# Reordering the seam between a mixture-of-experts layer, a four-group attention chain and a sparse key-value feed-forward

## The chip, the cores and the metric

The kernel runs as one launch on one core of a Trainium2 chip. The time is the device time of one execution in microseconds. It is given as the median of several runs of the unchanged kernel. All figures of a trace come from one further execution that the hardware profiler recorded.

## The reference, cut to what matters

The input `x` is 16 sequences of 128 tokens with 128 features, and `ctx_1024` has the same shape. Four layers follow each other. Each is a cross-attention over the context and a feed-forward part, and each adds its result to `x`. The change lies in the second half of layer 1 and in layer 2.

- Layer 1's feed-forward part is a mixture of 14 experts with one expert per token: `logits = norm(x) @ router`; each token goes to the expert with the largest logit; there `y = gelu(norm(x) @ w1[e] + b1[e]) @ w2[e] + b2[e]`; and `x += p * y`, with `p` the softmax weight of that expert.
- Layer 2's attention part is a block of its own: it normalises `x`, runs a causal self-attention, normalises, runs an attention over the context, normalises, runs a two-layer perceptron, normalises and adds to `x`. Its scores have one head of 128 features. A sequence's length is the number of scores of its first query that are not zero, and keys beyond that length are masked.
- Layer 2's feed-forward part looks up 1024 small experts: `xn = rms(x)`; `xn` gives 32 + 32 similarities for each of 8 heads; the eight best sums of one similarity of each side are kept per head; `x += (gelu(xn @ down.T) * weights) @ up`, with the kept sums as weights.

## The kernel before

Tokens lie on the 128 partitions. The 16 sequences form four groups of four (`NG = 4`, `GB = 4`), and X stays in SBUF for the whole program. A scheduler puts each engine's instructions into order at build time: it follows the order in which the Python code emits them, and among those it takes what its own cost estimates say is ready first. `tc.issue_after(ins)` adds an edge of order without a wait: what is emitted inside the block and runs on the engine of `ins` is issued behind `ins`.

The stretch in question is the function `layers_1_and_2`. Its pieces are Python generators. Each `next` emits a few instructions and stops at a `yield`, and the function chooses which piece is stepped next.

- `routing(n)` normalises a group, computes the router's logits and marks each token's expert (layer 1, groups 0 to 3).
- `places(k)`: the two halves of the batch (sets 0 and 1, two groups each) are sorted by expert. The function computes each token's row in a table in DRAM and issues eight scatters on GpSimd (line 1064), one per sequence.
- `tiles(k)`: the sorted table has 21 tiles of 128 rows, taken three at a time, so seven steps per set. Each step loads three tiles (`of`, line 1114, from SyncE's queue), copies three experts' weights by a register's value (`wt`, line 1123, on VectorE), runs two matrix products with a gelu between (lines 1134 to 1145), and stores the result (line 1148).
- `back(k)` gathers each token's result with eight indirect transfers on GpSimd (line 1155) and adds it to X on VectorE (line 1104). `biases(k)` adds the experts' second bias, with a small matrix product per group.
- `prepare(n)` computes the context products `k2` and `v2` of one group of layer 2's attention. `chain(n)`, called `attention` by the function that steps it, is the whole attention block of one group, in 34 steps: moments, normalising, query, scores and softmax (`weights`), weighted values, normalising, scores and softmax against the context, values, normalising, perceptron, and the final addition (line 1349). Its reciprocal root runs on GpSimd (line 245). The first two chains take other engines for small sums than the last two, which get `aside`.
- `layer2_ffn`: a prelude multiplies `w_q` with `keys` (`pk`, 16 products, line 1373). `begin(n)` normalises a group and transposes it. `similar(i)` and `thresholds` find the eight best sums of a sequence `i` per head. Then for each of 16 sequences and 8 heads one step builds a grid of 1024 sums on GpSimd (`C`, line 1446), marks the eight best on VectorE (line 1467) and adds the transposed grid into PSUM on TensorE (line 1469). There are 128 such steps. The grids have nine buffers and are emitted four steps ahead.

In the order before, `biases(0)` follows `places(1)` beside the last tiles of set 0. The gathers of set 0 are emitted after that scatter, with no edge between them, and the seven tiles of set 1 are stepped together with a round of `back(0)`, two chains side by side and all four `prepare`, and `biases(1)`. After the tiles, `back(1)` is stepped with the two chains. The prelude of the feed-forward part is emitted, then what is left of both chains. Chains 2 and 3 are stepped one step per head step. `begin(n + 1)` is called at the start of sequence `4n + 1`, and `similar(4n + 4)` at head step 6 of sequence `4n + 2`.

## Time and profile before

| | |
|---|---|
| median of 3 runs | 1454.21 us (1449.42 to 1455.87) |
| the profiled execution | 1458.99 us, span 1457.2 us, mean granted TensorE clock 0.883 |
| TensorE matmul busy | 1196.4 us (82%) |
| TensorE weight load busy | 812.1 us (56%) |
| VectorE busy | 867.9 us (60%) |
| ScalarE busy | 595.6 us (41%) |
| GpSimd busy | 497.0 us (34%) |

The busy shares are means over stages that have different limits, so they do not say what a stage is worth. The stretch of this change runs from about 792 us to 1275 us of the span. A timeline gives an instruction's start and length in us, its engine, its line, what it writes and reads, and in brackets how long the engine had been idle and what it then waited for. Matrix products are issued from one helper (line 232), so they are told apart by the tiles that they write.

### The profile page before, as it was taken

What the parts mean: (1) busy time and instruction counts of PE and PEld (TensorE: products, weight loads), DVE (VectorE), ACT (ScalarE), POOL (GpSimd) and SP (SyncE); (2) the same over time, 40 slices, a digit from 0 to 9 for tenths busy, and PEclk for the clock granted to TensorE, in tenths of its full rate; (3) what the DMA queues carried; (4) which work ended last, traced back from release to release, by engine and by line L of the source; (5) the groups of instructions that cost most, each with busy time, mean ns of one, the idle gap of its engine ahead of it and who ended that gap; (6) DMA issues with size and microseconds to landing.
All of it is one profiled execution on the core that took longest, in us unless ns stands there. A gap on an engine that the chain in (4) does not pass through costs nothing. (4 is left out here: it accounts for less than half of the span.)

```text
span 1457.2 us, 24584 instructions
## 1 busy us (share of the span) xinstructions
PE 1196.4 (82%) x9908; PEld 812.1 (56%) x9948; DVE 867.9 (60%) x2249; ACT 595.6 (41%) x1009; POOL 497.0 (34%) x559
## 2 busy tenths in 40 slices
PE   6887799898989777998777485677998898879986
PEld 2445355454545423555556374567887788825466
DVE  6666456565655676756545222347876888676652
ACT  3444465564655334445433236333334321133331
POOL 3223000000000135544322302169887899742100
PEclk9998799999999877979898578669999999999996
DMA  7000000000000200000012203000000000000000
GB/s 226 2 2 18 0 0 1 0 1 0 1 1 0 81 28 1 2 2 2 2 54 68 60 24 105 1 1 1 1 2 1 10 1 1 1 6 2 2 2 29
DMA packets 27587, 27.06 MB, mean 19 GB/s; under 512 B 3409, under 2 KB 25809, under 8 KB 27089
## 3 DMA queue, kind: packets, MB, share of 16 engines
q1 hardware_dynamic: 22128, 22.08, 4.6%
q0 software_dynamic: 1024, 2.10, 0.5%
q10 hardware_dynamic: 4320, 1.31, 0.4%
q8 instruction: 78, 1.28, 0.4%
q14 instruction: 37, 0.30, 0.1%
HBM read 17.88 MB, written 7.60 MB: 17 GB/s over the span
## 5 line engine op out<-in xcount | busy, mean ns | idle before, releaser
L1446 POOL TENSOR_TENSOR C<-sim 128x1024 f32<-128x1024 f32 x128 | 241.6, 1919 | 26.7 <-PE pc L1469 14.4
L1467 DVE MATCH_REPLACE8 C<-out,C 128x1024 f32<-128x1024 f32 x128 | 154.1, 1209 | 0.0
L232 PE MATMUL pc<-hm,weights_f 128*128 128x512 f32 x320 | 148.3, 595 | 3.0 <-DVE hm L840 2.6
L245 POOL TENSOR_TENSOR rstd<-ve,minus_half 128x4 f32<-128x4 f32 x44 | 44.7, 1017 | 291.8 <-DVE ve L242 277.0
L1469 PE MATMUL pc<-consts,C 128*128 128x128 f32 x1024 | 135.6, 284 | 10.3 <-POOL C L1446 6.2
L1469 PEld LDWEIGHTS pc<-consts,C 128*128 128x128 f32 x1024 | 122.9, 148 | 19.4 <-POOL C L1446 10.9
L461 DVE TENSOR_REDUCE nm<-s 128x8 f32<-128x1024 f32 x96 | 114.0, 1216 | 23.9 <-PE s L232 23.4
L354 POOL MEMSET V<- 128x2560 f32 x6 | 13.4, 2259 | 250.1 <-PE pb L934 236.7
L525 DVE RECIPROCAL inv<-av 128x128 f32<-128x128 f32 x48 | 45.9, 957 | 87.3 <-PE av L232 87.3
L232 PEld LDWEIGHTS pc<-hm,weights_f 128*128 128x128 f32 x320 | 59.9, 190 | 55.5 <-issue 45.7
L605 ACT ACTIVATE pT<-st 128x1024 f32<-128x1024 f32 x64 | 62.3, 1022 | 67.4 <-PE st L232 67.4
L232 PE MATMUL st<-Qb,K 32*128 32x512 f32 x512 | 84.9, 660 | 0.0
L232 PE MATMUL s<-Kb,Q 32*128 32x512 f32 x384 | 75.3, 690 | 6.6 <-ACT pT L533 2.6
L535 POOL TENSOR_TENSOR E<-pT 128x1024 f32<-128x1024 f32 x32 | 60.6, 1910 | 55.8 <-ACT pT L533 55.8
L475 POOL CAST nms<-nm 128x16 bf16<-128x16 f32 x64 | 14.7, 256 | 160.1 <-DVE nm L461 132.5
L232 PEld LDWEIGHTS av<-pT,V 128*32 128x32 f32 x1536 | 42.7, 116 | 39.9 <-issue 24.2
L840 DVE TENSOR_TENSOR hm<-he,M 128x512 f32<-128x512 f32 x64 | 40.7, 685 | 31.2 <-ACT he L836 28.3
L232 PE MATMUL av<-pT,V 128*32 128x128 f32 x1536 | 57.6, 291 | 1.6 <-DVE inv L549 1.2
L533 ACT ACTIVATE pT<-st 128x1024 f32<-128x1024 f32 x32 | 31.3, 1022 | 61.2 <-PE st L232 61.1
L232 PE MATMUL av<-pT,consts 128*32 128x128 f32 x1536 | 53.5, 280 | 0.0
L232 PE MATMUL ph<-xnext,weights_f 128*128 128x256 f32 (+1 forms) x96 | 32.1, 457 | 24.1 <-DVE xnext L893 24.1
L1123 DVE COPY wt<-weights_f 128x514 f32 x42 | 17.6, 426 | 55.7 <-PE po L232 50.6
(365 smaller groups left out, 2637.6 us busy)
## 6 DMA issues: line engine op xcount, KB each, us to landing
weights_f<-in_f SPq DMA_DIRECT2D x1, 3852.5 KB, 11.9
weights_f<-in_f SPq DMA_DIRECT2D x1, 2816.5 KB, 9.7
rows<-zero SPq DMA_DIRECT2D x2, 1344.0 KB, 15.5
of<-rows SPq DMA_DIRECT2D x14, 192.0 KB, 2.5
outs<-rT SPq DMA_DIRECT2D x14, 192.0 KB, 2.0
weights_f<-in_f SPq DMA_DIRECT2D x1, 2351.5 KB, 11.5
X<-in_x ACTq DMA_DIRECT2D x4, 256.0 KB, 9.2
ctx_sb<-in_ctx SPq DMA_DIRECT2D x4, 256.0 KB, 5.6
```

The source lines that it names most:

```text
L232: return nc.tensor.matmul(o, lhsT=lhsT, rhs=rhs, start=start, stop=stop)
L245: nc.gpsimd.tensor_tensor(o, ve, minus_half[:, :w], ALU.pow)
L461: nc.vector.tensor_reduce(nm[:, b, 8 * u : 8 * u + 8], ss[u].rearrange("p r (g k) -> p (r g) k", g=4), AX.X, ALU.max, negate=True,)
L525: nc.vector.reciprocal(y, s)
L533: nc.scalar.activation(E, st, AF.Exp, scale=8.0**-0.5)
L535: nc.gpsimd.tensor_mul(E2, E, E)
L605: nc.scalar.activation(pT, st, AF.Exp)
L840: nc.vector.tensor_mul(hm[:, k, c : c + 2, :], he, M[:, k, c : c + 2, :])
L1123: nc.vector.tensor_copy(wt, table[:, bass.ds(where[r], EW)])
L1446: nc.gpsimd.tensor_add(C, sim[:, h, 0, :].unsqueeze(2).to_broadcast(sh), sim[:, h, 1, :].unsqueeze(1).to_broadcast(sh),)
L1467: nc.vector.match_replace(at, m8[:, h, :], at, 0.0)
L1469: nc.tensor.matmul(pc[:, k // 4, k % 4 * P : (k % 4 + 1) * P], lhsT=C[:, 4 * k : 4 * k + 4, :].rearrange("p i j -> p (i j)"), rhs=ident, s ...
```

## The change

- `back` emits its eight gathers inside an `issue_after` on the last scatter of set 1, so the gathers of set 0 are queued behind that scatter on GpSimd. They are now emitted before `biases(0)`.
- `biases(0)` moves from beside set 0's last tiles to behind those gathers, followed by `prepare(0)` to `prepare(2)`. Then the first step of set 1's tiles is emitted, and then the additions of set 0.
- Each of the other six tile steps of set 1 is followed by three steps of chain 0 and, in the last three, by one step of chain 1. The weights of layer 2's feed-forward part are loaded after that, in two transfers, of which the first holds `w_q` and `keys`.
- The gathers of set 1 are emitted, and `biases(1)`, `prepare(3)` and the additions of set 1 are stepped with seven steps of chain 0.
- The prelude's products are followed by what is left of chain 0 (seven steps), each with a step of chain 1; on TensorE these are queued behind the prelude.
- What is left of chain 1 (22 steps), chain 2 and chain 3 are stepped beside the 128 head steps, one per step and two in one step of eight. Chain 1 gets `aside` as chains 2 and 3 do.
- `begin(n + 1)` moves from the start of sequence `4n + 1` to head step 5 of sequence `4n + 2`, one head step ahead of `similar(4n + 4)`.
- One `yield` in `weights` is gone, so a chain has 32 steps where it had 34.

```diff
-    def load(name):
+    def load(name, parts=()):
...
-        nc.sync.dma_start(t[:, :n], packs[name])
+        cut = [0, *parts, n]
+        for a, b in zip(cut, cut[1:]):
+            nc.sync.dma_start(t[:, a:b], packs[name][:, a:b])
...
+                d["scattered"] = ins
...
-            for at in range(ST):
-                nc.gpsimd.indirect_dma_start(
...
+            with tc.issue_after(state[1]["scattered"]):
+                for at in range(ST):
+                    nc.gpsimd.indirect_dma_start(
...
             nc.vector.tensor_scalar(top, most, -0.1 * BIG, -scale, ALU.max, ALU.mult)
-            yield
             E = tokens("E", 3)
...
-        def chain(n, aside=None):
+        def chain(n, complete, aside=None):
...
+            complete[n] = True
             yield
...
-            mm(pk[:, c * 32 : (c + 1) * 32], w["w_q"][:, c * P : (c + 1) * P],
-               w["keys"][:, c * 32 : (c + 1) * 32])
+            last = mm(pk[:, c * 32 : (c + 1) * 32], w["w_q"][:, c * P : (c + 1) * P],
+                      w["keys"][:, c * 32 : (c + 1) * 32]).ins
...
+        complete["prelude"] = last
...
         def begin(n):
+            assert n in complete
...
             pc = opened(i)
-            if i % GB == 1 and i + GB < NB:
-                begin(i // GB + 1)
...
                 if h == 4:
                     G = gelus(i)
+                if h == 5 and i % GB == 2 and i + GB < NB:
+                    begin(i // GB + 1)
                 if h == 6 and i + 2 < NB:
                     sims[i + 2] = similar(i + 2)
...
-                for _ in together(first, after(routing(NG - 1), places(1), biases(0))):
+                for _ in together(first, after(routing(NG - 1), places(1))):
                     pass
...
-                contexts = [prepare(n) for n in range(NG)]
-                half = together(
-                    attention(0), attention(1), after(*contexts)
-                )
-                second, others = tiles(1), back(0)
+                complete = {}
+                chains = [attention(n, complete, eps if n else None) for n in range(NG)]
+                second, sums = tiles(1), back(0)
+                one(sums)
+                for _ in after(biases(0), prepare(0), prepare(1), prepare(2)):
+                    pass
                 one(second)
-                one(others)
-                for _ in together(second, after(others, pairs(half)), biases(1)):
+                for _ in sums:
                     pass
-                load("f2")
-                others = back(1)
-                one(others)
-                for _ in range(6):
-                    one(half)
-                for _ in others:
-                    one(half)
+                for k in count():
+                    if not one(second):
+                        break
+                    steps(chains[0], 3)
+                    if k > 2:
+                        steps(chains[1], 1)
+                load("f2", [sum(cols["f2"][k][2] for k in ("w_q", "keys"))])
+                sums = back(1)
+                one(sums)
+                for part in (biases(1), prepare(3)):
+                    for _ in part:
+                        steps(chains[0], 1)
+                steps(chains[0], 1)
+                for _ in sums:
+                    steps(chains[0], 1)
             with tc.tile_pool(name="f2w", bufs=2, side="right") as wk:
-                forward = layer2_ffn(wk)
+                forward = layer2_ffn(wk, complete)
                 one(forward)
-                for _ in half:
-                    pass
-                chains = after(attention(2, eps), attention(3, eps))
-                for _ in forward:
-                    if chains and not one(chains):
-                        chains = None
-                        load("a3")
+                with tc.issue_after(complete["prelude"]):
+                    for _ in chains[0]:
+                        steps(chains[1], 1)
+                rest = after(*chains[1:])
+                for at, _ in enumerate(forward):
+                    for _ in range(2 if at % 8 == 3 else 1):
+                        if rest and not one(rest):
+                            rest = None
+                            load("a3")
```

`one(part)` emits one step of a generator, and `steps(part, n)` emits `n`.

More of the change, by code (lines that the diff above doesn't have):

```diff
@@ L1 @@
 import math
+from itertools import count
 from contextlib import ExitStack, nullcontext
@@ L1153, in back @@
             gs = [wk.tile([P, GB, P], F32, name="g", bufs=2) for _ in range(2)]
-            for at in range(ST):
-                nc.gpsimd.indirect_dma_start(
-                    out=gs[at // GB][:, at % GB, :], out_offset=None, in_=d["outs"][:, :],
-                    in_offset=bass.IndirectOffsetOnAxis(ap=d["place"][:, at : at + 1], axis=0),
-                )
+            with tc.issue_after(state[1]["scattered"]):
+                for at in range(ST):
+                    nc.gpsimd.indirect_dma_start(
+                        out=gs[at // GB][:, at % GB, :], out_offset=None, in_=d["outs"][:, :],
+                        in_offset=bass.IndirectOffsetOnAxis(ap=d["place"][:, at : at + 1], axis=0),
+                    )
             yield
@@ L1351, in chain, with layer2_ffn @@
                 )
+            complete[n] = True
             yield
         return prepare, chain
-    def layer2_ffn(wk):
+    def layer2_ffn(wk, complete):
         w = {k: sb[f"f2.{k}"] for k in cols["f2"]}
@@ L1539, in together, with steps @@
                 yield
+        def steps(part, n):
+            for _ in range(n):
+                one(part)
         def after(*parts):
@@ L1543, in after @@
                 yield from part
-        def pairs(part):
-            while one(part):
-                one(part)
-                yield
         with ExitStack() as left:
@@ L1575, in layers_1_and_2 @@
                 )
-                contexts = [prepare(n) for n in range(NG)]
-                half = together(
-                    attention(0), attention(1), after(*contexts)
-                )
-                second, others = tiles(1), back(0)
+                complete = {}
[4 more added lines that the diff above has]
+                    pass
```

## The prediction

> **What bounds the kernel now.** I read the page's slices first: TensorE is busy 7 to 9 tenths almost everywhere, with one dip in slices 23 to 27, where PE shows 4 to 8 and PEclk 5 to 8. So I cut that stretch by its events (last router result, first and last tile of set 1, last gather, end of chains 0 and 1, first marked grid, end of chain 3, last grid) and asked the table of windows. Columns: length; busy us (instructions) of PE, PEld, DVE, ACT, POOL; clock; DMA.
>
> ```profile
> 792.00:817.30 25.30, 6.30 (x25) 4.97 (x25) 12.03 (x55) 0.37 (x1) 17.78 (x18) 0.51 0.20 59
> 817.30:853.00 35.70, 30.07 (x122) 23.29 (x123) 8.71 (x22) 13.08 (x35) 2.53 (x2) 0.60 0.16 45
> 853.00:889.70 36.70, 29.20 (x204) 24.10 (x204) 8.07 (x21) 22.02 (x47) 0.00 (x0) 0.99 0.27 95
> 889.70:905.30 15.60, 6.76 (x32) 5.48 (x32) 5.45 (x30) 6.60 (x25) 8.72 (x9) 0.77 0.17 48
> 905.30:946.40 41.10, 26.30 (x121) 20.84 (x122) 10.89 (x62) 17.44 (x50) 5.68 (x7) 0.67 0.00 1
> 946.40:975.50 29.10, 21.38 (x100) 16.74 (x101) 10.45 (x72) 11.71 (x38) 14.25 (x10) 0.65 0.00 0
> 975.50:1162.70 187.20, 163.06 (x1216) 147.36 (x1227) 145.74 (x478) 70.29 (x168) 159.96 (x94) 0.92 0.01 3
> 1162.70:1274.80 112.10, 99.30 (x788) 94.25 (x794) 89.84 (x274) 15.75 (x30) 98.57 (x57) 0.94 0.01 2
> ```
>
> The first six rows, 183.5 us, are bound by latency: no engine is full, and TensorE runs at 0.51 to 0.67 of its clock in four of them. The last two are the 16 sequences of the feed-forward part, where PE, DVE and POOL are all at 78 to 89%. The first nine sequences, which carry chains 2 and 3, take 187.2 / 9 = 20.8 us each, the last seven 16.0.
>
> The timeline shows why the first row is empty:
>
> ```profile
> 797.32 0.15 DVE L1060 CAST place<-pos 128x8 uint32<-128x8 f32 x1
> ...
> 801.83 0.95 POOL L1155 DMA_INDIRECT g<-outs,place  x1 [0.30 <-issue]
> ...
> 803.08 1.13 POOL L1064 DMA_INDIRECT rows<-xn,place  x1 [0.30 <-DVE X L1104]
> ...
> 812.31 0.97 POOL L1064 DMA_INDIRECT rows<-xn,place  x1 [0.30 <-issue]
> ...
> 817.33 0.87 PE L1127 MATMUL pt<-consts,of 128*128 128x128 f32 x3 [15.74 <-DMA of<-rows]
> ```
>
> The places are known at 797.5, but set 0's gathers hold POOL until 802.8, so the scatter that TensorE waits for starts at 803.1. The seam after the tiles:
>
> ```profile
> 889.17 0.56 DVE L1147 COPY rT<-po 128x384 f32<-128x384 f32 x1 [8.04 <-PE po L232]
> ...
> 901.83 0.49 DVE L252 BATCH_NORM_STATS2 st<-pz 128x6 f32<-128x128 f32 x2
> ...
> 946.50 6.90 PEld L232 LDWEIGHTS pk<-weights_f 128*128 128x128 f32 x32 [4.25 <-DVE X L1349]
> ...
> 965.50 7.51 POOL L1446 TENSOR_TENSOR C<-sim 128x1024 f32<-128x1024 f32 x4 [0.71 <-ACT sim L1414]
> ...
> 975.59 1.21 DVE L1467 MATCH_REPLACE8 C<-out,C 128x1024 f32<-128x1024 f32 x1
> ```
>
> The chains' moments at 901.8 sat in DVE's queue behind additions that waited for gathers. The prelude `pk` came only after both chains, and the first grid is marked 86.4 us after the last tile.
>
> **The change part by part.** The base is the profiled execution, 1458.99 us (span 1457.2). It lies 4.8 above the median of the runs, so I take the difference off the median.
>
> *Scatter.* With the gathers behind it, the scatter starts 0.3 after its places instead of at 803.1: 5.3 us earlier. `biases(0)` also leaves the stretch in which DVE computes the places; its two additions at 794.9 and 797.1 waited in that queue, worth up to 2.5 more. So 5.3 to 7.8; I take 7. The gathers then run about 806 to 816, and chain 0's first reciprocal root behind them at about 816.6; before it came at 813.3 behind the scatter, and its normalising ran at 821.9, so nothing on the path is later.
>
> *Tile stage* (817.3 to 889.7, 72.4 us). Out go four `prepare` (pk at 850.1 and 862.8, pv at 852.9 and 865.6: 2 to 4 us of PE each, some 11 in all) and `biases(1)` (831.1 to 834.5 and 838.7 to 846.4, about 5 of PE). Three `prepare` and `biases(0)` fill PE's 15.7 us wait. In comes chain 0's second half instead of chain 1's first, about the same work. Set 0's tiles at full clock came every 4.7 us (line 1147 at 779.3 and 784.0), which for seven is 33; three chain steps between two tiles, some 2 to 3 us of PE and ACT, make it 44 to 54. If the clock stays where it was, the stage can stay at 72 or, with chain waits in PE's queue, grow by a few us (I allow 4). I take 54, near the row of set 0's tiles, since PE no longer stands still before: 18 us gained, bounds -4 and 28.
>
> This term rests on the clock: the row 817 to 853 had PE busy 30.1 of 35.7 us at 0.60, so 30.1 x 0.4 = 12 us of it is slow clock. [...]
>
> *Last tile to first marked grid* (889.2 to 975.6, 86.4). The gathers and additions after the last tile still take 16 us (889.2 to 905.2); chain 0's steps 19 to 25 fit in it. From the moments to chain 0's last addition the trace has 901.8 to 946.4 for one and a half chain halves of two chains side by side; counted for one chain from moments of the context part on (rows 928.8 to 946.4, 17.6 us), it stays about 17.5, as half the queue is gone but the chain is a string of waits. `pk`, 7.0 us on PE, moves into DVE's and ACT's part of that (moments, root, normalising: 5.5 us); what sticks out, 1.5, I add. Behind it `begin(0)` no longer waits for `keys` (953.6) and `whole`: moments 1.9, small sums and root 2.4, normalising 1.6, transposition and copy 1.3, two products 4.0, copy 0.6, then 965.5 to 975.6 unchanged, 22 in all where the trace has 29. Sum 16 + 17.5 + 1.5 + 22 = 57; seven steps of chain 1 beside it, 3 us. So 60: 26 gained. Bounds 10 (chain 1's steps and `pk` fully in the way) and 35.
>
> *Feed-forward part* (299 us). It now carries 86 chain steps for 68, or 0.69 of a chain more. Chains 2 and 3 cost 9 x (20.8 - 16.0) = 43 us, or, against sequences 9 to 14 (101.6 / 6 = 16.9), 35: 17 to 22 per chain. So 12 to 15 more; I take 13.
>
> *Late `begin`.* Its cover was 13 head steps; now it is one. The rows of `begin(2)`:
>
> ```profile
> 1065.81 1.12 DVE L1349 SCALAR_TENSOR_TENSOR X<-pz,rstd,X 128x128 f32<-128x128 f32 x4 [4.13 <-POOL rstd L245]
> ...
> 1069.13 0.47 DVE L252 BATCH_NORM_STATS2 st<-X 128x6 f32<-128x128 f32 x2
> ...
> 1082.11 0.69 ACT L1389 ACTIVATE xT<-pt,weights_f 128x512 f32<-128x512 f32 x1 [3.66 <-PE pt L293]
> ```
>
> From moments to `xT` are 13.7 us, to the similarities about 16, against some three head steps (7 us) until DVE has their maxima in its queue. The markings of the current sequence sit behind those maxima. Left over are 0 to 9 us per group, three times 0 to 27; with grids computed ahead on POOL and most maxima emitted late, I take 6.
>
> *Small edits.* The two-part load costs one more issue on SP, hidden: the weights were asked for at 874.9 and used at 946.5. The dropped `yield`, and chain 1's `aside` (its small sums go from DVE to ACT, which is 38% busy in the row with chains), I take at nothing; bounds -2 and +3, for without that slack ACT delays the chain, not the grids.
>
> Sum: -7 - 18 - 26 + 13 + 6 = -32: 1427 on the profiled execution, 1422 on the median.
>
> **The rivals.** (a) *The slow clock stays and the gain shrinks.* Tile stage 66 instead of 54, chain 0 as slow as two were: -7 - 6 - 18 + 13 + 6 = -12, so 1442. For it: the clock fell to 0.6 even in busy windows. Against: set 0's tiles ran at 1.00 after a full stretch.
>
> (b) *Slower: `begin` holds the marking queue.* Chain 1 must end before `begin(1)`. Chain 2 took from 961.8 to 1066.9 for 32 steps, 3.3 us each, while head steps without chains take 2.0. Where DVE stands at each of three group changes for the whole 16 us of `begin` and similarities, that is 48; with 13 for the steps it is 61 against a front gain of 51, or of 31 as in (a): +10 to +30, 1464 to 1484. It decides from about 13 us per group change on. For it: `[4.13 <-POOL rstd]` shows such a stand. Against: POOL holds grids ahead, and the order is chosen by readiness.
>
> (c) *It doesn't do what it says*: the scheduler already places chain steps where engines are free, and the tiles stay bound by ScalarE's gelu hand-offs; only the scatter's 7 and the seam's low bound of 10 remain, and the feed-forward part takes 13 back: -4, so 1450.
>
> **How the numbers follow.** Forecast 0.57; its best ends (tile stage 44, seam 35, no late `begin`: -7 - 28 - 35 + 12 = -58, 1396) another 0.06; (a) 0.13; (c) 0.08; (b) 0.16. This measurement can tell about 0.5%, 7.3 us, from no change, so faster means below 1446.9. The forecast, its best end and most of (a) are faster, 0.74; (c) with 0.01 of (a) same, 0.09; (b) with 0.01 of (a) slower, 0.17. The forecast's own range is 1400 to 1442. For 8 in 10 I take 1394 to 1458: under it some 0.05 is left out, above it most of (b).
>
> **What would show it.** Right: the last scatter ends near 805 and the first product of set 1 starts near 810; line 1147's last copy near 863; `pk` before chain 0's last addition; the first marked grid near 924; sequences 0 to 9 of the feed-forward part near 21 us each, its length near 318. Wrong: a granted clock near 0.6 between 810 and 850 (a); DVE idle behind `sim` or `rstd` for over 10 us at sequences 3, 7 and 11 (b).

## The result, and the profile after

The changed kernel takes 1459.47 us in the median of 10 runs (1455.8 to 1466.1), the kernel before 1451.01 in 10 (1444.73 to 1455.87). The ratio is 1.006, with a 95% interval of 1.0039 to 1.008: slower by 0.6%, where 1422 was forecast. The profiled execution took 1462.37 us, its span is 1460.6 us, 3.4 more than before. A single profiled execution of each kernel shows where time goes; how much is gained or lost is read from the medians.

This is the table of windows of the changed kernel, cut at the same events as the first table of the prediction (columns as there: length; busy PE, PEld, DVE, ACT, POOL; clock; DMA):

```profile
792.00:810.30 18.30, 13.85 (x56) 9.44 (x55) 7.60 (x27) 3.88 (x7) 10.62 (x11) 0.63 0.19 56
810.30:842.00 31.70, 22.49 (x129) 19.39 (x130) 11.57 (x41) 12.83 (x35) 8.04 (x8) 0.73 0.23 65
842.00:875.50 33.50, 20.97 (x131) 18.03 (x131) 7.42 (x24) 23.81 (x57) 2.27 (x2) 0.83 0.06 18
875.50:894.30 18.80, 10.12 (x49) 7.55 (x47) 7.02 (x24) 4.57 (x12) 7.78 (x8) 0.68 0.53 192
894.30:925.10 30.80, 24.02 (x100) 19.47 (x100) 8.17 (x37) 9.37 (x26) 2.72 (x4) 0.60 0.00 1
925.10:946.00 20.90, 11.99 (x58) 8.08 (x58) 5.69 (x52) 6.17 (x17) 11.11 (x7) 0.76 0.00 1
946.00:1187.00 241.00, 197.29 (x1418) 175.70 (x1419) 167.69 (x564) 90.15 (x231) 181.27 (x108) 0.89 0.00 1
1187.00:1281.90 94.90, 85.99 (x690) 79.77 (x689) 77.28 (x239) 13.53 (x27) 83.46 (x49) 0.95 0.02 5
```

The first six rows are 154.0 us, where the first six before were 183.5: the front did become some 30 us shorter. The last two are 335.9 us where they were 299.3. By stage, each measured between events in the profiled executions:

| us | before | after | difference | forecast |
|---|---|---|---|---|
| last tile of set 0 to first product of set 1 | 27.8 | 20.6 | -7.2 | -7 |
| to the last tile of set 1 | 71.8 | 64.7 | -7.1 | -18 |
| to the first marked grid | 86.4 | 71.0 | -15.4 | -26 |
| feed-forward part | 299.2 | 335.9 | +36.7 | +19 |
| all else | 972.0 | 968.4 | -3.6 | 0 |

The timeline of the changed kernel shows the head and the first tile:

```profile
796.60 1.03 POOL L1067 DMA_INDIRECT rows<-xn,place  x1 [19.75 <-DVE X L1108]
...
810.29 0.52 PE L1131 MATMUL pt<-consts,of 128*128 128x128 f32 x3 [1.33 <-DMA of<-rows]
...
818.02 0.35 DVE L1108 SCALAR_TENSOR_TENSOR X<-g,prob,X 128x128 f32<-128x128 f32 x1 [0.67 <-DMA g<-outs,place]
...
818.96 0.15 DVE L245 TENSOR_SCALAR ve<-mv 128x4 f32<-128x4 f32 x1
...
819.20 1.05 POOL L248 TENSOR_TENSOR rstd<-ve,minus_half 128x4 f32<-128x4 f32 x1 [2.69 <-DVE ve L245]
...
820.48 0.88 ACT L277 ACTIVATE x<-X,low,rstd 128x128 f32<-128x128 f32 x2 [6.11 <-DVE low L275]
...
821.66 0.79 PE L235 MATMUL po<-wt,h 128*128 128x128 f32 x2 [4.78 <-ACT h L1141]
```

The scatter and the first product came where the forecast had them. Then chain 0's moments stand in VectorE's queue between the additions, which wait for the gathered rows, the last until 818.0. The root on GpSimd comes at 819.2: GpSimd has been idle for 2.7 us and waits for VectorE's `ve`. ScalarE stands 6.1 us at chain 0's normalising, the second pair of the first tile's gelus is queued behind that, and TensorE waits 4.8 us for it. The first tile takes 14.8 us instead of 10.0.

The seam, in the same timeline:

```profile
883.84 1.02 SPq L208 DMA_DIRECT2D weights_f<-in_f  x2
...
889.99 0.35 DVE L1108 SCALAR_TENSOR_TENSOR X<-g,prob,X 128x128 f32<-128x128 f32 x1 [4.10 <-DMA g<-outs,place]
...
894.42 1.28 ACT L1267 ACTIVATE E<-E,total 128x128 f32<-128x128 f32 x4 [5.57 <-DVE total L1265]
...
906.54 0.69 DVE L1381 COPY keys<-pk 128x512 f32<-128x512 f32 x1 [5.64 <-PE pk L235]
```

The load of the weights started only when `biases(1)` had read the old contents of their buffer: SyncE waited 7.9 us for its product `pb`, which ends at 883.8. The last gathers landed beside it, and chain 0's softmax scaling stood in VectorE's queue behind the additions that wait for them. Later VectorE stood 5.6 us at the copy of `pk`, with chain 0's moments behind it.

The growth of the feed-forward part is best read on VectorE, which marks all grids. Its busy time there went from 235.5 to 244.9 us and its idle time from 63.7 to 90.9: of 36.7 us, 9 are work and 27 are waits. The longest single wait, 10.5 us, ends the first sequence, while chain 1 runs beside the first grids:

```profile
954.78 7.51 POOL L1453 TENSOR_TENSOR C<-sim 128x1024 f32<-128x1024 f32 x4
...
963.29 0.85 ACT L273 ACTIVATE low<-minus,rstd 128x1 f32<-128x1 f32 x4 [10.21 <-POOL rstd L248]
...
964.54 0.48 PE L1286 MATMUL pt<-consts,x 128*128 128x128 f32 x1 [9.51 <-ACT x L277]
...
968.87 0.47 DVE L1430 MAX8 best<-sim 128x8 f32<-128x32 f32 x4 [10.52 <-ACT sim L1421]
```

Chain 1's root stands on GpSimd behind four grids. ScalarE waits for it, TensorE waits for the normalised tile, and the next sequence's similarities, on which VectorE depends, are queued behind. Here is one change of sequence in the changed kernel, 6 to 7, VectorE first, then ScalarE, then GpSimd:

```profile
1090.58 1.21 DVE L1474 MATCH_REPLACE8 C<-out,C 128x1024 f32<-128x1024 f32 x1
...
1103.72 0.23 DVE L1442 MAX8 m<-sums 128x8 f32<-128x64 f32 x1 [3.88 <-POOL sums L1435]
...
1112.69 0.09 DVE L1474 MATCH_VALUE_LOAD C<-out,C 128x8 f32 x1 [7.79 <-ACT out L1446]
1102.68 0.85 ACT L273 ACTIVATE low<-minus,rstd 128x1 f32<-128x1 f32 x4 [4.50 <-POOL rstd L248]
...
1109.16 0.85 ACT L273 ACTIVATE low<-minus,rstd 128x1 f32<-128x1 f32 x4 [1.96 <-POOL rstd L248]
...
1112.41 0.24 ACT L1446 ACTIVATE out<-m 128x64 f32<-128x64 f32 x1
1096.03 5.64 POOL L1453 TENSOR_TENSOR C<-sim 128x1024 f32<-128x1024 f32 x3
1101.63 1.02 POOL L248 TENSOR_TENSOR rstd<-ve,minus_half 128x4 f32<-128x4 f32 x1
...
1108.11 1.02 POOL L248 TENSOR_TENSOR rstd<-ve,minus_half 128x4 f32<-128x4 f32 x1
```

No grid is marked for 22 us. Chain 2's last steps, the moments of chain 3 and of `begin(2)`, and the thresholds of sequence 7 meet here. The maxima are done at 1104.9, but the scaling `out`, on which the marks depend, stands on ScalarE behind two normalisings: chain 3's first, whose root (1101.6) stands on GpSimd behind three grids, and that of `begin(2)`, whose root (1108.1) comes only after that. These are two kinds of VectorE's waits over the whole part (us in total, times, longest); before, the same two were 4.3 and 6.7:

```profile
DVE best L1430 <- ACT sim L1421: 16.2, 5, 10.5
...
DVE C L1474 <- ACT out L1446: 11.7, 11, 7.8
```

With the wait for GpSimd's sums (18.1 before, 23.1 after), the waits at changes of sequence grew from 29.1 to 51.0 us, 22 of the 27. Two single waits, the 10.5 and the 7.8 shown, are 18 of them. This says where VectorE stood, not what it cost: e11 below waits 45.1 us at these three places, and its feed-forward part is 3 us shorter than before.

### The profile page after: what moved, and what is told of

Read it like the earlier page. It is cut to its first block, busy times and chain, and to the rows that moved or that the text cites. A ratio compares the mean times of both kernels' runs of the same rounds, so it can differ in the third digit from the quotient of the medians.

```text
span 1460.6 us, 24623 instructions
## 1 busy us (share of the span) xinstructions
PE 1198.2 (82%) x9948; PEld 809.8 (55%) x9948; DVE 869.3 (60%) x2242; ACT 602.8 (41%) x1030; POOL 496.4 (34%) x559
## 5 line engine op out<-in xcount | busy, mean ns | idle before, releaser
L1476 PEld LDWEIGHTS pc<-consts,C 128*128 128x128 f32 x1024 | 121.5, 147 | 14.6 <-issue 7.7
L478 POOL CAST nms<-nm 128x16 bf16<-128x16 f32 x64 | 14.7, 255 | 157.6 <-DVE nm L464 133.1
L843 DVE TENSOR_TENSOR hm<-he,M 128x512 f32<-128x512 f32 x64 | 40.8, 686 | 31.1 <-ACT he L839 28.3
L235 PE MATMUL po<-wt,h 128*128 128x128 f32 x168 | 38.7, 330 | 22.3 <-ACT h L1141 22.1
L235 PE MATMUL ph<-xnext,weights_f 128*128 128x256 f32 (+1 forms) x96 | 32.1, 457 | 24.1 <-DVE xnext L896 24.1
## 6 DMA issues: line engine op xcount, KB each, us to landing
rows<-zero SPq DMA_DIRECT2D x2, 1344.0 KB, 14.8
```

What stands on the lines that cost most here:

```text
L235: return nc.tensor.matmul(o, lhsT=lhsT, rhs=rhs, start=start, stop=stop)
L478: nc.gpsimd.tensor_copy(at[:, b, :, :, 0], of[:, b])
L843: nc.vector.tensor_mul(hm[:, k, c : c + 2, :], he, M[:, k, c : c + 2, :])
L1476: nc.tensor.matmul(pc[:, k // 4, k % 4 * P : (k % 4 + 1) * P], lhsT=C[:, 4 * k : 4 * k + 4, :].rearrange("p i j -> p (i j)"), rhs=ident, s ...
```

## The experiments

"Front" is the time from the last tile of set 0 to the first marked grid, "FF" the feed-forward part, "idle" VectorE's idle time in FF, all in the profiled executions. The ratio is to the kernel before, run on the same chip, with its 95% interval. Two cautions belong to the table. Before, e1 and e3 run the same instructions in the same order in FF on each engine, and their FF is 299.2, 299.5 and 295.0: a difference of up to 4.5 us between single executions shows nothing. And e13 to e15 ran on a chip on which the kernel before took 1445.1 us in the median, where it took 1450.1 to 1452.5 for the others, so that their ratios may lie some 0.4% high beside the rest.

| kernel | ratio | front | FF | idle |
|---|---|---|---|---|
| before | 1 | 186.0 | 299.2 | 63.7 |
| after | 1.006 [1.0039, 1.008] | 156.3 | 335.9 | 90.9 |
| e1 head alone | 1.0002 [0.9987, 1.0018] | 182.3 | 299.5 | 64.0 |
| e2 e1, late `begin` | 0.9977 [0.9959, 0.9996] | 183.2 | 296.0 | 60.2 |
| e3 scatter first | 1.0015 [0.9999, 1.0031] | 185.3 | 295.0 | 59.5 |
| e4 after, no late roots | 0.9897 [0.9866, 0.9928] | 153.2 | 309.6 | 58.0 |
| e5 before, no late roots | 0.9853 [0.9815, 0.989] | 181.9 | 274.2 | 40.1 |
| e6 chains behind gelu | 1.003 [1.0007, 1.0053] | 156.4 | 335.8 | 90.9 |
| e7 root on VectorE | 1.0568 [1.0524, 1.0611] | 157.9 | 407.7 | 92.9 |
| e8 seam, emission moved | 1.0047 [1.0024, 1.0071] | 157.3 | 333.7 | 88.7 |
| e9 e2, steps spread | 0.9983 [0.9957, 1.0009] | 186.0 | 295.9 | 61.4 |
| e10 e2, 3 steps in 2 | 1.0186 [1.0145, 1.0226] | 182.6 | 322.0 | 82.5 |
| e11 before, spread | 0.9975 [0.9951, 1.0] | 182.5 | 295.9 | 61.4 |
| e12 after, chain 1 ahead | 1.0095 [1.0062, 1.0129] | 197.1 | 295.5 | 59.7 |
| e13 after, single steps | 1.015 [1.0108, 1.0193] | 159.3 | 332.0 | 90.3 |
| e14 e2, doubled steps | 1.0161 [1.012, 1.0203] | 183.9 | 314.9 | 71.2 |
| e15 e2, root as sqrt | 0.9944 [0.992, 0.9969] | 183.6 | 280.7 | 43.0 |
| e16 e2, chains late | 1.0061 [1.0035, 1.0087] | 179.5 | 309.3 | 74.9 |
| e17 after, half chain 1 | 1.0069 [1.004, 1.0099] | 173.3 | 323.5 | 83.0 |
| e18 e15, sums on VectorE | 0.9813 [0.9776, 0.985] | 178.8 | 271.8 | 19.4 |

### The front: e1, e3, e6, e8

e1 takes the change's head alone and keeps the paired chains, `begin` and one chain step per head step of before:

```diff
+                half = together(attention(0, complete), attention(1, complete), prepare(3))
+                for _ in together(second, pairs(half), biases(1)):
```

> The head of the change alone: gathers of set 0 behind set 1's scatter, biases and three context preparations ahead of set 1's tiles; the two chains, the feed-forward part and the calls of begin as in the kernel before. Theory (the head is a gain, the loss lies in the feed-forward part): set 1's first product near 810, the feed-forward part near 299 us as before, 6 to 15 us faster in all. Rival (the head loses what it gains, because chain 0's normalising waits on ScalarE behind the gathers and holds the tiles' gelu): within 4 us of the kernel before.

The scatter started 6.9 us behind set 0's last tile (13.5 before) and the first product 21.2 (27.8). The tile stage grew from 71.8 to 80.8, its first tile from 10.0 to 14.6, and the time did not move. e3 is the kernel before with the edge only:

```diff
+            with tc.issue_after(state[1]["scattered"]):
+                for at in range(ST):
```

> The kernel before with one edit: set 0's gathers queued behind set 1's scatter. If the scatter is what the tiles wait for and nothing else comes late: 5 us faster. If chain 0's reciprocal root, now behind the gathers on GpSimd, holds ScalarE's queue and with it the tiles: 0 to 2 us faster.

Its first product came 5.5 us earlier, its first tile took 14.0, and its ratio is one within the interval. So an earlier scatter alone gains nothing here. In its trace, too, chain 0's root waits 2.0 us for VectorE's `ve`, and ScalarE stands 4.7 us at the normalising, ahead of a pair of gelus: what the scatter gives is taken back behind the later gathers. e6 queues the chain steps of the tile stage behind the tile's last gelu:

```diff
+                    with tc.issue_after(marks["gelu"]):
+                        steps(chains[0], 3)
```

> The changed kernel, with what the chains run on ScalarE beside set 1's tiles queued behind the last gelu of the tile just emitted. Theory (chain 0's normalising, which waits for a root behind the gathers, stands ahead of the first tile's gelu, and exponentials between gelus reload tables): first tile 10 to 11 us where it took 14.8, tile stage 54 to 58 where it took 64.7, and 5 to 9 us less in all. Rival (the tiles are held by the slow clock): stage 62 or more, nothing gained.

The first tile fell to 11.8 us, but others grew, and the stage stayed at 64.6 (64.7 after). The order on ScalarE inside a tile is not what bounds the stage. e8 puts `biases(1)` ahead of the load and the copy of `pk` behind chain 0's second remaining step:

```diff
+                for _ in biases(1):
+                    steps(chains[0], 1)
                 load("f2", [sum(cols["f2"][k][2] for k in ("w_q", "keys"))])
...
+                        if k == 1:
+                            one(forward)
```

> The changed kernel with two edits at the seam: biases(1) ahead of the load of the feed-forward part's weights, and the copy of keys emitted behind chain 0's normalising. In the changed kernel the load started at 883.8, when biases(1) had read its weights, and the gathers landed 4 us late beside it; the copy waited 5.6 us for pk in VectorE's queue ahead of chain 0's moments. Theory: last tile to first marked grid 62 to 65 us where it took 71, 5 to 8 us less in all, if the feed-forward part keeps its 336. Rival (chain 0 is held by TensorE's queue behind pk and chain 1's products): 69 or more.

The seam went from 71.0 to 69.6 us, but the run does not test the two waits, for both are still there:

```profile
887.37 0.82 SPq L208 DMA_DIRECT2D weights_f<-in_f  x2
...
908.90 0.69 DVE L1383 COPY keys<-pk 128x512 f32<-128x512 f32 x1 [5.56 <-PE pk L235]
```

The scheduler put the copy ahead of the rest of chain 0's moments again, and the load started 9.9 us behind the last tile, where it was 8.9. Moving the emission did not move these two in their queues. What these two waits cost the seam is open.

### Late begin: e2

```diff
-            if i % GB == 1 and i + GB < NB:
-                begin(i // GB + 1)
+                if h == 5 and i % GB == 2 and i + GB < NB:
+                    begin(i // GB + 1)
```

> As e1_head_alone, and begin moved to head step 5 of sequence 4n + 2, one head step ahead of similar; chains as before. Theory (the late begin holds VectorE's queue): 15 to 25 us slower than e1_head_alone, in sequences 3, 7 and 11. Rival (the loss comes from carrying chain 1 beside the head steps): 0 to 5 us slower than e1_head_alone.

The feed-forward part is 3.5 us shorter than in e1, within the spread of single executions. A late `begin` costs nothing where the chain of its group has ended long before (here 17 head steps or more).

### The place of the root: e4, e5, e7

In e4 (on the changed kernel) and e5 (on the kernel before), which both leave out the root itself:

```diff
+        if aside is not None:
+            nc.vector.reciprocal(o, ve)
+        else:
             nc.gpsimd.tensor_tensor(o, ve, minus_half[:, :w], ALU.pow)
```

> The changed kernel, with the reciprocal roots of chains 1 to 3 and of begin taken off GpSimd: VectorE takes a plain reciprocal in their place, so the root itself is left out. Theory (chain 1's roots queue behind the grids on GpSimd, and TensorE then waits for the normalised tile): the feed-forward part falls from 336 to some 310 to 318 us, 18 to 26 us faster than the changed kernel. Rival (the loss is the plain work of 0.7 of a chain and of the late begin): 5 us faster at most, GpSimd's 10 us of roots being hidden.

> The kernel before, with the roots of chains 2 and 3 and of begin taken as plain reciprocals on VectorE, as in e4_root_dve (the root itself is left out). e4's feed-forward part took 309.6 us. If roots behind grids cost every chain alike (some 6 to 8 us per chain), this one falls from 299 to 283 to 289 us and the kernel by 10 to 16. If they hurt only the changed order, where chain 1's first root meets the first run of grids: 295 to 299 us, and the kernel within 4 us of before.

FF fell by 26.3 us in the one and by 25.0 in the other. So a root on GpSimd, queued behind grids, is dear in both orders; it does not make most of the difference between them, which stays 35.4. (In e4 8.5 of that is one cast that ran long, shown at the end; without it 27 are left of 36.7.) e7 computes the true root on VectorE (a guess from the bits and two Newton steps, eight small instructions):

```diff
+            nc.vector.tensor_single_scalar(g, ve.bitcast(I32), 1, ALU.logical_shift_right)
...
+            for k in range(2):
+                nc.vector.tensor_mul(t, y, y)
```

> The changed kernel, with the roots of chains 1 to 3 and of begin computed on VectorE in full: a first guess from the bits and two Newton steps, eight instructions of 128x4 where GpSimd ran one. Thirteen roots at eight times about 0.16 us add 17 us to VectorE's queue. Theory (it is the wait in GpSimd's queue that costs, not the work): feed-forward part 310 to 320 us, 15 to 24 us faster than the changed kernel. Rival (VectorE is as full as GpSimd, and the added work is on the path): 325 or more, under 10 us gained.

It was 5.7% slower. Groups of VectorE's instructions in its feed-forward part, shapes kept apart (busy, mean ns):

```profile
L255 DVE TENSOR_TENSOR t<-g 128x4 f32<-128x4 f32 x28 | 19.7, 702 | 0.0
L252 DVE TENSOR_SCALAR g<-g 128x4 int32<-128x4 int32 x14 | 14.5, 1035 | 0.0
```

Instructions on four columns took 0.4 to 1.0 us each in the mean of their group, and VectorE's busy time rose from 245 to 315 us. The timeline shows that they are not slow by themselves. Here is the same instruction ahead of all grids and beside them, with GpSimd's row behind it:

```profile
926.38 0.16 DVE L255 TENSOR_TENSOR t<-g 128x4 f32<-128x4 f32 x1
...
956.68 1.81 DVE L255 TENSOR_TENSOR t<-g 128x4 f32<-128x4 f32 x1
954.68 13.11 POOL L1465 TENSOR_TENSOR C<-sim 128x1024 f32<-128x1024 f32 x7
```

The 77 instructions of these roots that no GpSimd instruction overlaps took 0.12 to 0.17 us each. Those beside one took up to 1.85 us, nearly the length of a grid. So the trade was not GpSimd's wait against VectorE's work: a small instruction beside a grid could take nearly as long as the grid, and the root has eight.

### The number, density and place of the chain steps: e9 to e14, e16, e17

e9 spreads the 68 steps of e2 over five of six head steps (`if at % 6 != 5 and chains and not one(chains)`). e11 does the same to the kernel before, with the late `begin`. e10 makes them denser: `for _ in range(1 + at % 2)`.

> As e2_head_late_begin (296 us of feed-forward part), with the 68 steps of chains 2 and 3 spread over five of every six head steps instead of every one. Theory (engines' queues tie head steps to chain steps, and a chain step takes 2.7 us wherever it stands, a head step alone 2.0): 68 x 2.7 = 185 us for 82 head steps, then 46 x 2.04 = 94: 279 us, some 17 us faster than e2. Rival (a chain step costs fixed work, 0.6 us, wherever it lies): 294 to 298 us.

> The kernel before, with the late begin and the spread of e9_spread, and nothing else of the change. Theory: its feed-forward part falls from 299 to about 279 us, the kernel 15 to 20 us faster than before. Rival (fixed work per step): within 4 us of before.

> As e2_head_late_begin, with three chain steps to two head steps. Theory (the chain sets the pace): 185 us for 45 head steps, then 83 x 2.04 = 169: some 350 us, 50 us slower than e2; less if a chain step gets shorter with fewer head steps between. Rival (fixed work per step): 294 to 300 us.

Spread, FF stays at 295.9 in both (296.0); at three steps in two head steps it is 322.0. So fewer steps per head step than one are worth nothing, more cost. In e10 the chains' ends move as well as the density. e14 gives e2 the change's own density, two steps in one head step of eight:

```diff
+                for at, _ in enumerate(forward):
+                    for _ in range(2 if at % 8 == 3 else 1):
```

> The changed head, the two paired chains of the kernel before, the late begin, and chains 2 and 3 stepped with two steps in one of eight head steps as in the change (its 68 steps then take 60 head steps), where the same kernel with one step per head step took 296.0 us in the feed-forward part. Theory (density): the part grows by 15 to 20 us, to 310 to 316, and the time against the kernel before is 1.007 to 1.012. Rival (the price lies with chain 1 and the first sequences, not in the doubled step): the part takes 294 to 300, and the time is 0.995 to 1.001 of the kernel before.

FF grew by 18.9 us. But 8.4 of these are one instruction: the cast of layer 3's mask, which the scheduler places here, took 1.8 us in e2 and 10.2 in e14 (more on it at the end). The density is worth some 10. e13 takes the doubled steps out of the changed kernel, with three steps of chain 1 more ahead:

```diff
-                        steps(chains[1], 1)
+                        steps(chains[1], 2 if k < 3 else 1)
...
-                    for _ in range(2 if at % 8 == 3 else 1):
+                    if rest and not one(rest):
```

> The changed kernel with three steps of chain 1 more before the first sequence (two beside each of chain 0's first three remaining steps), and then one chain step per head step throughout, 83 steps for 86 and none doubled. Theory (what makes a chain step dear is that two stand in one head step of eight, so that they come denser than one per head step): most of the 36.7 us by which the feed-forward part grew goes, and it takes 310 to 320 us, where the changed kernel took 335.9. Rival (the price comes with chain 1 itself: its root stands in the first run of grids and delays the first sequences): the part takes 328 to 333, the three steps' own price less. The seam grows by 0 to 4 us in both. The time against the kernel before: 0.985 to 0.995 by the theory, 1.000 to 1.004 by the rival.

FF fell by 3.9 us only, which is within the spread of single executions. But e13 changes the place as well. Chains 2 and 3 now end when 57 and 93 grids are marked (56 and 87 in the change), and the normalising of their groups' `begin` comes at 64 and 96 marks, a whole sequence later than the change's 56 and 88. So e13 does not tell what the doubled steps cost in the change. e12 ends chain 1 ahead of the feed-forward part and spreads the rest over four of five head steps:

```diff
-                        steps(chains[1], 1)
-                rest = after(*chains[1:])
+                        steps(chains[1], 3)
+                    for _ in chains[1]:
+                        pass
+                rest = after(*chains[2:])
...
+                    if at % 5 != 4 and rest and not one(rest):
```

> The changed kernel with chain 1 emitted to its end before the head steps, three steps to one of chain 0's last seven, and chains 2 and 3 in four of five head steps. Theory: the first marked grid comes 10 to 26 us later than the changed kernel's, the feed-forward part takes 64 x 2.7 + 48 x 2.04 = 271 us where it took 336, and the kernel is 20 to 35 us faster than before. Rival (fixed work per step): feed-forward part 295 to 300, 10 us faster than before at most.

FF is 295.5 again, 40.4 less, and the front 197.1, 40.8 more. So 22 more steps of chain 1 cost 40.8 us of the front. The 40.4 of FF are not chain 1's price only, as the doubled steps went too. In the kernel before, in step with chain 0, the front with both was only 30 us longer than the changed kernel's with chain 0 and ten steps of chain 1. e17 moves 12 steps of chain 1 more ahead than the change does (in e13, `steps(chains[1], 3 if k < 5 else 2)`), and leaves 10:

> The changed kernel with 19 steps of chain 1 beside chain 0's last seven (the change has 7), and one chain step per head step, so 74 steps in the feed-forward part, of which 10 are chain 1's. Chains 1, 2 and 3 then end after some 10, 42 and 74 head steps, eleven ahead of the begin of the group. Theory (pile-up): the part falls from 332 us (83 single steps) to 298 to 306, that is 296 for 68 steps and 0.5 to 0.9 us for each of six more. Rival (the price lies with chain 1's presence in the first sequences): 310 to 325, half of chain 1's price still being there. The seam grows by 8 to 16 us over the changed kernel's 71. By the theory the time against the kernel before is 0.980 to 0.992, by the rival 0.995 to 1.005.

FF is 323.5, 27 us above e2 with ten steps of chain 1 more. Its first sequence (first mark to the scaling behind the eighth) takes 25.9 us, where it takes 14.0 in e2 and in before; in the changed kernel it takes 28.5, and in e4, without the late roots, 16.2. In e13, with chain 1 only three steps further, it takes 14.2, and yet FF is hardly shorter. e16 changes only the place: it starts chains 2 and 3 of e2 17 head steps later (`if at > 16 and chains and not one(chains)`), so that they end close to `begin`: in the trace a chain's last addition comes 11 and 5 us ahead of the normalising of its group's `begin`, in the change 9, 13 and 9 for chains 1 to 3. (By the code it is three head steps and one here, and two, six and ten in the change.)

> The kernel with the late begin (changed head, paired chains 0 and 1, one chain step per head step, 296.0 us in the feed-forward part), in which chains 2 and 3 only start after 17 head steps. The same 68 steps are stepped at the same density, and chain 1 is not among them; but chain 2 now ends and chain 3 starts within three head steps of begin(2), and chain 3 ends just ahead of begin(3), as in the change. Theory (a pile-up: a chain's end, the begin of its group, the next chain's start and the similarities meet at one change of sequence and hold the engines' queues in a row, as in the 22 us without a marking at 1091 to 1113 of the changed kernel): the feed-forward part takes 308 to 320 us, and the time against the kernel before is 1.005 to 1.013. Rival (the place of a chain's end does not matter, only the number of steps, their density and chain 1): 293 to 300 us, 0.995 to 1.000.

The same steps at the same density, without chain 1, cost 13.3 us more, all of it VectorE's idle time (14.7). The worst change of sequence, 11 to 12, has 19.6 us between two marks. VectorE there:

```profile
1202.04 1.40 DVE L1431 MAX8 best<-sim 128x8 f32<-128x32 f32 x14 [8.31 <-ACT sim L1422]
...
1208.87 1.11 DVE L1443 MAX8 m<-sums 128x8 f32<-128x64 f32 x8 [5.04 <-POOL sums L1436]
```

The similarities wait for `begin(3)`, which waits for chain 3 (its last addition comes at 1189.5, the normalising of `begin(3)` at 1194.3), and the grids that GpSimd then works off stand ahead of the sums.

### A version that beats both: e15, e18

e15 is e2 with the whole root computed off GpSimd, and e18 also forms the sums of the thresholds on VectorE:

```diff
+            nc.vector.reciprocal(ve, ve)
+            nc.scalar.activation(o, ve, AF.Sqrt)
...
-            nc.gpsimd.tensor_add(
+            nc.vector.tensor_add(
                 sums, best[:, :, 0, :].unsqueeze(3).to_broadcast(sh),
```

> The same kernel as with the late begin (changed head, paired chains 0 and 1, one chain step per head step, 1448 us), in which chains 2 and 3 take their roots as a reciprocal on VectorE and a square root on ScalarE, where they had a power on GpSimd. The whole root is computed. Leaving the root out had saved 24 us in the feed-forward part of the kernel before. Theory (the root is dear because it stands behind grids in GpSimd's queue): the feed-forward part falls from 296 to 272 to 285 us, the table loads on ScalarE (1.28 us each, two per root, some 12 roots, on an engine that is idle for over half of that part) taking a part back, and the time against the kernel before is 0.980 to 0.992. Rival (ScalarE's table loads and VectorE's small reciprocals, up to 1 us each beside the grids, hold the similarities as much as GpSimd did): 292 to 305 us, 0.995 to 1.005.

> The kernel with the late begin and the root as a reciprocal on VectorE and a square root on ScalarE (280.7 us in the feed-forward part, 0.994 of the kernel before), in which the 64 sums of each head's best similarities, one instruction of 128x512 per sequence, are formed on VectorE and no longer on GpSimd. Theory (the changes of sequence set what is left above the busy time: VectorE's maxima waited 17.9 us for GpSimd's sums, which stand behind grids): those waits go, VectorE gains some 16 x 0.6 = 10 us of work, GpSimd loses 16; the part takes 268 to 278 us, and the time against the kernel before is 0.985 to 0.993. Rival (VectorE, busy for 238 of the 281 us, is the bound, so its added work costs what the waits gave): 279 to 290 us, 0.993 to 1.001.

e15 takes 1434.95 us in the median, 0.6% less than the kernel before, and e18 1424.12, 1.9% less. The table of windows of e18 over its feed-forward part:

```profile
960.40:1232.24 271.84, 253.52 (x2040) 229.14 (x2041) 252.49 (x791) 104.71 (x230) 243.61 (x128) 0.99 0.01 3
```

VectorE is busy for 252 of 272 us, TensorE for 254 and GpSimd for 244, at a clock of 0.99. The sums cost VectorE 1.30 us each in the mean, 19.5 in all, and took away 24 us of its idle time. Once the waits for GpSimd's sums are gone, three engines are busy for about 90% of the part or more; which of them bounds it was not tried. Both edits stand on the order of before in the chains; the change's order is not needed for it, and what the two edits together give in the change's order was not tried.

## Why the prediction was wrong, point by point

- **Scatter, -7: right** by its own measure (-7.2 to the first product). The step "nothing on the path is later" failed. The gathers ended at 816.5 as said, but the root came at 819.2 and not at 816.6, since it waited for moments that stand between the additions on VectorE. The normalising is not later in time (820.5, before 821.9), but the first product is 7 us earlier, so it now stands ahead of a pair of the first tile's gelus and holds TensorE for 4.8 us. In e1 and e3 nothing of the gain is left in the time.
- **Tile stage, -18: measured -7.** The clock argument was half right: it rose from 0.60 to 0.73 in the first 32 us, but fell from 0.99 to 0.83 in the rest. TensorE's busy time fell from 59.3 to 43.5 us and the stage by 7, so TensorE's speed is not its bound after the change. The tile was priced at set 0's 4.7 us plus the work of three chain steps; the chain's waits, which lie in the same queues as gelu and `po`, were priced at nothing. That they make the difference is argued: e6 took one order of them away without a gain, and no run takes the chain out of the stage. That the clock comes back once TensorE no longer stands still ahead of the tiles was the author's guess, and these rows do not test it: at 0.63 and 0.73 over 50 us, TensorE was busy for 13.9 of 18.3 and for 22.5 of 31.7 us, with the 4.8 us above as one gap.
- **Seam, -26: measured -15.4.** Gathers and additions 18.8 (16 forecast), `begin` to first mark 20.9 (22 forecast: right), and between them 30.8 where 22 was forecast. Two steps failed. Chain 0's steps up to the context part's moments were to fit beside the gathers; its softmax scaling stood behind the additions, and the moments began at 899.9, 5.6 us after the 894.3 of the last addition. From them to the end of the last addition the trace has 25.2 us where the sum had 17.5 for chain 0, kept from two chains side by side, and 4.5 for `pk` and chain 1; there VectorE stood 5.6 us at the copy of `pk`. What the seam would take without these waits is open, as e8 left them in place.
- **Feed-forward, +13: the term that decides.** The step that failed is the price of a chain step: it was taken as work, 17 to 22 us per chain from before's mean. A chain's price there is largely VectorE's waiting, and this depends on where the steps stand: the same 68 steps cost 296 us of FF (e2, e9), 309 (e16), 315 (e14) or 322 (e10). Chain 1's 22 steps at the old price would be 12 to 15 us; the 36.7 is 9 of work and 27 of waits. Three things are shown to cost something by themselves: the place of the steps (13 in e16), the doubled step (about 10 in e14) and chain 1 in the first grids (12 to 14.5 in the first sequence, of which the second makes up some 4). How the 27 us divide among them stays open: e13, without the doubled step and with a first sequence of 14.2, gave only 4, but put the `begin` of two groups a sequence later.
- **Late begin, +6:** nothing by itself (e2). In the change a chain's last addition comes only 9 to 13 us ahead of the normalising of its group's `begin`, where in e2 it is 42 and 27 for chains 2 and 3; what the late call costs there was not tried apart, as `begin` cannot stand ahead of its chain's end. Rival (b) had this mechanism and its condition, "Chain 1 must end before `begin(1)`"; it was given 0.16. Its price of 13 per group change was met once in the changed kernel (22 us between two marks at sequence 6 to 7), not three times. Its sign, VectorE idle for over 10 us behind `sim` or `rstd`, appeared at the first change of sequence and not at 3, 7 and 11.
- **Rival (a)** had the front's numbers right: tile stage 66 (64.7 measured), seam 68 (71.0). Its mechanism, the slow clock, was there in part only (0.73 and 0.83 in the tile stage, not 0.6), so the closeness is partly luck. With it the forecast would have been 1442; the rest of the miss is the feed-forward part.
- **The small edits**, taken at nothing, were not run alone: chain 1's `aside`, the dropped `yield`, the load in two parts. ScalarE's busy time in the feed-forward part rose from 86 to 104 us, so `aside` at nothing is not shown. A chain of the kernel before has 34 steps and not the 32 of rival (b), which makes a step 3.1 us and not 3.3.
- **The signs.** Right were the scatter near 805, the first product near 810 and `pk` ahead of chain 0's last addition (899.6 against 923.9). Wrong were the last copy (874.95 for 863), the first marked grid (945.99 for 924), the sequences 0 to 9 (24.1 us each for 21) and the part's length (335.9 for 318).

## What to carry to other kernels

Work that is moved from a latency-bound front into a part with full engines isn't priced by its busy time or by the mean of what already stands there: look where its hand-offs meet the hand-offs of that part, and count them on the engine that the part hangs on. A chain moved so that it ends just ahead of what needs it takes away the slack on which a late consumer lives. Small instructions on the engine with the longest instructions (roots and sums behind 1.9 us grids) were the cheapest thing to move: two such edits, with the changed head and the late `begin`, gave 1.9%, while the whole reordering lost 0.6%. Where they go matters as much: eight small instructions on VectorE for each root lost 5.7%. And an edit of the emission order is only an experiment when the trace shows that the queues changed.

## What the runs showed of the hardware

One cast on VectorE, 128x512 fp32 to bf16, took 0.41 us in e9, 0.42 in e13, 0.41 in e17 and 10.2 us in e14. VectorE's and GpSimd's timeline of e14:

```profile
1191.07 10.22 DVE L1619 CAST m_causal<-consts 128x512 bf16<-128x512 f32 x1
1189.78 11.23 POOL L1454 TENSOR_TENSOR C<-sim 128x1024 f32<-128x1024 f32 x6
```

It ended at 1201.3, 0.3 us behind a run of six grids on GpSimd without a gap. In e4 it was 9.0 us beside such a run and again ended 0.3 us behind it. It did not last to the end of a run each time, though. In the kernel before, the second cast of this shape began inside the first of two grids and ended 0.3 us behind that one:

```profile
1169.88 1.09 DVE L1608 CAST m_causalT<-consts 128x512 bf16<-128x512 f32 x1
1168.78 3.97 POOL L1446 TENSOR_TENSOR C<-sim 128x1024 f32<-128x1024 f32 x2
```

The markings, 128x1024, kept their 1.21 us throughout. The cast shown of the kernel before took 1.09 us, and e7's small instructions at most 1.85 beside grids of 1.87 in the mean (13.11 for seven, above), against 0.12 to 0.17 where no GpSimd instruction overlaps: none of them longer than about one grid. In e4 and e14 the cast lasted through five and six grids in a row, not one. What decides between the two was not shown.
